# C turned in place, two groups' terms on GpSimd, and unread products in a scan layer

## The chip, the cores and the metric

The kernel runs on one core of one Trainium2 chip. A core has a matrix engine (TensorE, PE in the profile), three engines for element-wise work (VectorE or DVE, ScalarE or ACT, GpSimd or POOL), a queue engine that only issues transfers here (SyncE or SP), two kinds of memory near the engines (SBUF, and PSUM, into which TensorE writes), and DMA engines that move data to and from DRAM. Each engine works through its own list of instructions in order, and engines wait for one another by semaphores.

The metric is the device time of one execution in microseconds, as the median of several. A profiled execution leaves one record for nearly every instruction, and the span is the time from the first of them to the last.

## The reference, cut to what matters

The model is a chain of four layers on an image of 48 x 48 tokens with 768 channels: an attention block, a spectral layer, a scan layer, and a spectral layer again. The change touches the scan layer alone:

```python
B = silu(x @ W_B + b_B + B_bias)           # N = 64 channels x R = 4, per token
C = silu(x @ W_C + b_C + C_bias)
X = silu(x @ W_X + b_X)
alpha, gamma = sigmoid(x @ W_dec + b_dec), sigmoid(x @ W_lam + b_lam)
theta = x @ W_th + b_th
for i in range(12):
    inj = rope(B, theta * (i + 1)) * X
    H = conv3x3(H) + conv_b                # depthwise: one 3x3 filter per channel
    H = alpha * H + inj                    # i == 0
    H = alpha * H + (1 - gamma) * alpha * prev + gamma * inj
    prev = inj
out = silu((rope(C, theta * 12) * H) @ W_out + b_out)
```

`rope` turns pairs of channels by an angle: (a cos - b sin, a sin + b cos). Since the angle grows by theta from one iteration to the next, the sum of the terms that are added to H obeys a recurrence, s(i+1) = 2 cos(theta) s(i) - s(i-1), so that only the first two of them, `s0` and `s1`, are worked out by turning.

## The kernel before, in words

`scan_phase` holds the layer. Tokens lie on 112 of the 128 partitions (two image rows in 48 partitions each, the second at partition 64), so that the 48 rows make 24 pair-rows (`NPR`).

**Projections** (L1204 to L1294). A loop over eight column groups `q` takes three pair-rows each. For each pair-row, TensorE multiplies the tokens by all the weights (L1223): 357 columns (C, alpha, theta, X, gamma) and 256 columns (B), over six chunks of input channels, into one of three PSUM tiles `pss[0..2]`. Three of the six chunks come from `xh`, a tile that holds half of the layer's input for all tokens; the others come from tiles that `rows_back` makes. VectorE adds biases into two SBUF tiles, `za` (two buffers) and `g` (L1224). ACT applies silu to X, B and C (L1234), takes sin and cos (L1198, L1199) and sigmoids (L1250, L1251); each change of function costs a table load. VectorE turns B (`turn`, L1425, six operations with two temporaries `m0` and `m1`), writes the first H (L1260) and works out `s0` and `s1` (L1288, L1289, L1293, L1294), with ACT's products `u` (L1270). C, which is a part of `za`, and the cos and sin of 12 theta are written to DRAM (`c_d`, L1263, L1264). The last group's operations are held in program order by `pin`.

**Around the seam.** After the last group `x_close` gives back the memory of `xh` and of the projection weights. The output weights `wo`, `bo`, the filters `bands` of the groups 1 to 7 (group 0 has its own, loaded early) and `alr`, alpha spread over R, lie in the memory that has become free. SP issues their transfers in order.

**Diffusion** (L1316 to L1370). Iterations 1 to 11 times eight groups of eight channels (`gr`) make 88 steps. `step` issues: 64 passes of TensorE with the filters as band matrices (L1323) into `pss[gr % 4]`; VectorE's product with alpha (L1325, called mult in the prediction); VectorE's addition of `s` into H (L1327, called H); GpSimd's product t = 2 cos(theta) s (L1331); ACT's copy of t into the same PSUM tile (L1332). `after`, one step later, issues VectorE's s <- t - s (L1343, called sub), which reads t from PSUM. In the last iteration there is no next term; there the turned C is read from DRAM and multiplied with H (L1349), on GpSimd for seven groups and on VectorE for the last. On three of each four steps one more operation is issued from `turns`: for each of the eight `q`, C and the cos and sin are read from `c_d` (L1357, L1358), turned by six GpSimd operations (L1425), and written to DRAM as `cr_d`.

**Order.** The order on each engine is settled when the program is built: a scheduler places ready instructions by priority, except where `tc.keep_in_program_order` holds them. `keep_warm` (L128 to L133) is a helper that another stage uses already: it issues matmuls whose result nobody reads.

Of the kernel before, what the change touches and what calls it, by code (L numbers as in the profile page):

```python
# [12 lines left out]
F32 = mybir.dt.float32  # L13
F32R = mybir.dt.float32r
AF = mybir.ActivationFunctionType
ALU = mybir.AluOpType
# [4 lines left out]
P = 128  # L21
# [1108 lines left out]
def scan_phase(tc, ident, w, wts, rows_back, xh, x_close, c_d, cr_d, out_open):  # L1130
# [13 lines left out]
    nc = tc.nc  # L1144
    (b0_d, b1_d, cb_d, bands_d, wo_d, bo_d) = wts
    R4 = 3
# [8 lines left out]
    with tc.tile_pool(name="sc_s", bufs=1, side="left") as sp:  # L1155
# [9 lines left out]
        with (  # L1165
# [15 lines left out]
            with (  # L1181
# [27 lines left out]
                for q in range(NQ):  # L1209
# [50 lines left out]
                    V.tensor_tensor(H[:K, :, :, 1 + q * R4 : 1 + (q + 1) * R4], i03, over_r(ac, NN), ALU.add)  # L1260
                    pin(V.tensor_scalar(th, th, float(ITERS), None, ALU.mult))  # L1261
                    cs12 = sincos(th, q, "t12")
                    nc.sync.dma_start(c_d[:K, q, :NCR], c)  # L1263
                    nc.sync.dma_start(c_d[:K, q, NCR:].rearrange("p (s m) t -> p s m t", s=2), cs12)  # L1264
                    c1q = c1[:K, :, prs]
                    pin(V.tensor_scalar(c1q, cs[:, 0], 2.0, None, ALU.mult))

# [24 lines left out]
                    t1 = s1[:K, :, :, prs]  # L1292
                    V.tensor_tensor(t1, i03, over_r(bc, NN), ALU.mult)  # L1293
                    V.tensor_tensor(flat(t1), flat(t1), u, ALU.subtract)  # L1294
            x_close()
            wo, bo = out_weights()
            with (
# [5 lines left out]
                for gr in range(NG):  # L1303
# [2 lines left out]
                        nc.sync.dma_start(bands[:, (gr - 1) * GC : gr * GC], bands_d[:, ch])  # L1306
                    nc.scalar.copy(alr[:, ch], al[:, ch].unsqueeze(2).to_broadcast([P, GC, RR, NPR]))
                s = [s0, s1]
                half = GC * RR * NPR // 2

                def banks(v, gr):
# [2 lines left out]
                def step(it, gr):  # L1314

                    sc = s[it % 2]  # L1316
                    ch = slice(gr * GC, (gr + 1) * GC)
                    ps = pss[gr % 4]
                    for k in range(GC):
                        n = gr * GC + k  # L1320
                        cols = slice(k % 4 * RR * NPR, (k % 4 + 1) * RR * NPR)
                        for i, (r0, d) in enumerate(((0, 1), (HD, 1), (0, 0), (HD, 2))):
                            nc.tensor.matmul(ps[r0 : r0 + G, k // 4, cols], lhsT=bands[:, n - GC, i, :] if gr else bands0[:, n, i, :], rhs=H[:, n, :, d : d + NPR], start=i < 2, stop=i >= 2)  # L1323
                    pv = ps[:, :, :half]
                    V.tensor_tensor(pv, pv, banks(alr, gr), ALU.mult)  # L1325
                    by_bank = lambda v: v.rearrange("p (b n) r t -> p b (n r) t", b=2)
                    V.tensor_tensor(by_bank(H[:, ch])[:, :, :, 1 : 1 + NPR], pv.rearrange("p b (n t) -> p b n t", t=NPR), by_bank(sc[:, ch]), ALU.add)  # L1327
                    if it + 1 < ITERS:
                        t = tp.tile([P, GC, RR, NPR], F32, tag="t", name=f"t_{it}_{gr}")
                        m0 = (gr * GC) % NM  # L1330
                        GP.tensor_tensor(t, sc[:, ch], c1[:, m0 : m0 + GC].unsqueeze(2).to_broadcast([P, GC, RR, NPR]), ALU.mult)  # L1331
                        nc.scalar.copy(pv, t.rearrange("p (b n) r t -> p b (n r t)", b=2))  # L1332
                    else:
                        cr = tp.tile([P, NQ, GC * RR, R4], F32, tag="t", name=f"crg_{gr}")
                        nc.sync.dma_start(cr[:K], cr_d[:K, :, gr * GC * RR : (gr + 1) * GC * RR])
                        crs[gr] = cr

                def after(it, gr):

                    sn = s[(it + 1) % 2]  # L1340
                    if it + 1 < ITERS:
                        sb = banks(sn, gr)
                        V.tensor_tensor(sb, pss[gr % 4][:, :, :half], sb, ALU.subtract)  # L1343
                        return
                    nr = slice(gr * GC * RR, (gr + 1) * GC * RR)
                    hg = sn.rearrange("p n r t -> p (n r t)").rearrange("p (t n) -> p n t", t=NPR)
# [1 line left out]
                    by_q = lambda v: v.rearrange("p n (q t) -> p n q t", t=R4)  # L1348
                    (V if gr == NG - 1 else GP).tensor_tensor(by_q(hg[:K, nr]), by_q(Hd[:K]), crs[gr][:K].rearrange("p q n t -> p n q t"), ALU.mult)  # L1349

                def c_turned(q):


                    c, cr = (tp.tile([P, NCR, R4], F32, tag="t", name=f"{nm}_{q}")[:K] for nm in ("c", "cr"))
                    sc = tp.tile([P, 2 * NM, R4], F32, tag="sc", name=f"sc_{q}", bufs=2)[:K]
                    m = [tp.tile([P, NM, RR, R4], F32, tag=f"m{j}", name=f"m{j}_{q}", bufs=1)[:K] for j in range(2)]
                    nc.sync.dma_start(c, c_d[:K, q, :NCR])  # L1357
                    nc.sync.dma_start(sc, c_d[:K, q, NCR:])  # L1358
                    co, si = (sc[:, j * NM : (j + 1) * NM].unsqueeze(2).to_broadcast([K, NM, RR, R4]) for j in range(2))
                    yield from turn(GP, cr, c, co, si, m)  # L1360
                    yield lambda: nc.sync.dma_start(cr_d[:K, q], cr)

                crs = {}
                steps = [(it, gr) for it in range(1, ITERS) for gr in range(NG)]
                turns = (op for q in range(NQ) for op in c_turned(q))
                for i in range(len(steps) + 1):
                    if i < len(steps):
                        step(*steps[i])
                    if i % 4:
                        next(turns, int)()  # L1370
                    if i:
                        after(*steps[i - 1])
# [3 lines left out]
        with (  # L1376
# [24 lines left out]
            for half in range(2):  # L1401
                cols = slice(half * TB, (half + 1) * TB)
                for p2 in range(NPR // 2):
                    if half == 0 and p2 % 2 == 0:
                        turned(1, p2 // 2)
                    for t in range(2):
# [4 lines left out]
                        V.tensor_tensor(x3[:, pr, cols], ps[:K, :TB], bo[:, cols], ALU.add)  # L1411
                        nc.scalar.activation(x3[:, pr, cols], x3[:, pr, cols], AF.Silu)
                    yield


def turn(eng, out, in_, co, si, m):
# [12 lines left out]
def block_kernel(ctx: ExitStack, tc: tile.TileContext, a: dict):  # L1429
# [84 lines left out]
        return stack.enter_context(tc.tile_pool(name=name, bufs=1, side="right"))  # L1514

    wts = [a[k] for k in ("b_scan", "bias_scan", "conv_b", "bands", "W_out", "b_out")]
    c_d = dram.tile([P, 8, NN * RR + 2 * NM, 3], F32, tag="c_d", name="c_d")
    cr_d = dram.tile([P, 8, NN * RR, 3], F32, tag="cr_d", name="cr_d")

    def x_close():  # L1520
# [497 lines left out]
```

## Time and profile before

| | |
|---|---|
| median of 3 executions | 3582.45 us (3582.03 to 3585.97) |
| profiled execution | 3582.01 us, of it 3580.2 us span |
| busy: TensorE, VectorE, ACT, GpSimd | 3507.9, 2002.3, 1140.0, 679.5 us |
| projections, from about | 2823 us |
| last matmul of the projections, first of the diffusion | ends 2991.6, starts 3000.30 us |
| last matmul of the diffusion, about | 3247.2 us |

A line of a group reads: source line, engine, operation, output and inputs by the program's names, sizes, count, then busy time and mean duration in ns, then idle time of the engine just before and what ended it. A line of the instruction list reads: start in us, duration in us, engine, line, operation, and in brackets the idle time before it and what released it. A line of stretches reads: limits, length, then busy time with count of TensorE, its weight loads, VectorE, ACT and GpSimd, then the granted clock of TensorE (1 is full speed), the share of the DMA engines and GB/s. Records are pipelined: on VectorE the next instruction may start before the one ahead of it has ended, so a pace is read from starts.

### The profile page before, as it was taken

To read this page: it belongs to the slowest core of one execution; us is meant where nothing else is said; L and a number is where in the kernel's file an instruction comes from. 1 tells how busy PE (TensorE), PEld (TensorE's weight loads), DVE (VectorE), ACT (ScalarE), POOL (GpSimd) and SP (SyncE) were. 2 spreads that over 40 slices of the span, in tenths; PEclk is the share of its full clock that TensorE was granted. 3 is DMA by queue.
4 is the path that set the end of the run, shared out by engine and by line. 5 is a ranking of instruction groups with operands and counts; after the bars stand their busy time and mean duration, and the time that the engine had idled before them with its cause. 6 is when DMAs were issued, how large, how long until landed. Compare 5 with 4: busy or idle time off the path is not lost.

```text
span 3580.2 us, 52877 instructions
## 1 busy us (share of the span) xinstructions
PE 3507.9 (98%) x21238; PEld 2149.6 (60%) x21238; DVE 2002.3 (56%) x3015; ACT 1140.0 (32%) x1735; POOL 679.5 (19%) x566
## 2 busy tenths in 40 slices
PE   9999999999999999989999999999999998999997
PEld 5666554444444444555555555555578777996685
DVE  7644467776776776564243324232245478995454
ACT  1321255555555555103101210120023265223332
POOL 3211101111111110340000000000023303981131
PEclk9999999999999999999999999999999999999999
DMA  8555556655545443343346334534544403104356
GB/s 276 201 189 190 186 155 184 181 157 148 154 124 151 124 125 87 120 157 121 108 139 175 116 108 137 158 109 127 144 122 115 110 20 105 37 28 106 97 143 132
DMA packets 282167, 480.38 MB, mean 134 GB/s; under 512 B 39206, under 2 KB 235462, under 8 KB 275704
## 3 DMA queue, kind: packets, MB, share of 16 engines
q1 hardware_dynamic: 266568, 456.13, 43.9%
q10 hardware_dynamic: 15344, 20.75, 1.9%
q8 instruction: 171, 2.80, 0.3%
q14 instruction: 84, 0.69, 0.1%
HBM read 330.82 MB, written 145.98 MB: 133 GB/s over the span
## 4 chain that ended last, share of the span: by engine, by line
PE 90%; DVE 3%; DMA 3%; POOL 2%; ACT 1%; issue 1%; SPq 0%; ACTq 0%; POOLq 0%; DVEq 0%
PE p L996 14%; PE p L1059 13%; PE s L657 12%; PE av L688 12%; PE qk L375 6%; PE c L1223 4%; PE s L667 3%; PE c L1323 3%; PE v L180 3%; PE pj L180 2%; PE f_z L1666 2%; PE f_z L1667 2%; PE f_x L1631 2%; PE so L1410 2%; PE f_u L1682 2%; PE f_o L1645 1%
## 5 line engine op out<-in xcount | busy, mean ns | idle before, releaser
L677 DVE TENSOR_TENSOR acc<-acc,p 128x928 f32<-128x928 f32 (+1 forms) x480 | 561.1, 1169 | 258.8 <-ACT p L669 217.6
L669 ACT ACTIVATE p<-s 128x928 f32<-128x928 f32 (+1 forms) x540 | 505.9, 939 | 488.1 <-PE s L667 468.6
L657 PE MATMUL s<-qt,kv 64*128 64x464 f32 (+1 forms) x2160 | 520.8, 558 | 5.7 <-DMA qt<-q_d 5.7
L1059 PE MATMUL p<-w,h 128*128 128x384 f32 x1512 | 492.3, 487 | 0.0
L688 PE MATMUL av<-p,kv 128*64 128x464 f32 (+1 forms) x2160 | 442.6, 554 | 0.0
L1059 PEld LDWEIGHTS p<-w,h 128*128 128x128 f32 x1512 | 285.7, 190 | 198.8 <-issue 4.2
L667 PE MATMUL s<-bt,oneh 64*128 64x464 f32 (+1 forms) x1080 | 399.8, 729 | 0.8 <-DMA bt<-rh_d 0.8
L688 PEld LDWEIGHTS av<-p,kv 128*64 128x64 f32 x2160 | 147.0, 137 | 261.2 <-issue 248.8
L657 PEld LDWEIGHTS s<-qt,kv 64*128 64x128 f32 x2160 | 203.2, 187 | 162.0 <-issue 153.6
L996 PE MATMUL p<-x2nT,w 128*128 128x384 f32 x864 | 292.8, 489 | 4.2 <-POOL rr L1035 4.2
L1323 PE MATMUL c<-H,bands 128*48 128x96 f32 x5632 | 244.6, 247 | 10.9 <-DVE th L1261 8.3
L375 PE MATMUL qk<-xnT,wqk 128*128 128x384 f32 x756 | 249.8, 487 | 0.1
L1323 PEld LDWEIGHTS c<-H,bands 128*48 128x48 f32 x5632 | 234.8, 123 | 20.9 <-issue 8.7
L996 PEld LDWEIGHTS p<-x2nT,w 128*128 128x128 f32 x864 | 164.8, 191 | 120.8 <-POOL rr L1035 4.4
L996 PE MATMUL p<-xT,w 128*128 128x384 f32 x648 | 220.8, 486 | 0.0
L1035 POOL TENSOR_TENSOR rr<-rr,ml_b 128x1152 f32<-128x1152 f32 x12 | 31.8, 2649 | 944.7 <-DMA rr<-xr_d 828.3
L991 ACT ACTIVATE h<-h,ml_b 128x384 f32<-128x384 f32 x144 | 88.3, 614 | 345.8 <-DVE h L1011 173.6
L375 PEld LDWEIGHTS qk<-xnT,wqk 128*128 128x128 f32 x756 | 141.5, 190 | 93.1 <-issue 0.7
L1331 POOL TENSOR_TENSOR t<-s,c 128x768 f32<-128x768 f32 x80 | 144.4, 1828 | 180.8 <-DVE s L1294 168.2
L996 PEld LDWEIGHTS p<-xT,w 128*128 128x128 f32 x648 | 123.2, 190 | 85.8
L667 PEld LDWEIGHTS s<-bt,oneh 64*128 64x128 f32 x1080 | 106.8, 187 | 105.4 <-issue 103.3
L1666 PE MATMUL f_z<-f_w,f_o 97*96 97x96 f32 x800 | 134.2, 249 | 0.0
(334 smaller groups left out, 4594.0 us busy)
## 6 DMA issues: line engine op xcount, KB each, us to landing
w<-w1s_d SPq DMA_DIRECT2D x36, 768.0 KB
w<-w2s_d SPq DMA_DIRECT2D x36, 768.0 KB
w<-w1s_d SPq DMA_DIRECT2D x36, 576.0 KB
w<-in_mlp_w_dram SPq DMA_DIRECT2D x27, 768.0 KB
yu<-f_ys SPq DMA_DIRECT2D x48, 384.0 KB
wqk<-wqk_d SPq DMA_DIRECT2D x12, 1344.0 KB
bt<-rw_d SPq DMA_DIRECT2D x72, 174.0 KB
bt<-rh_d SPq DMA_DIRECT2D x72, 174.0 KB
```

Of the source, the lines that this page charges most:

```text
L180: nc.tensor.matmul(p[:, :TB], lhsT=rhs[n][:, c, t * P : (t + 1) * P], rhs=w[:, c, :], start=c == 0, stop=c == NC2 - 1)
L375: nc.tensor.matmul(p[:, :TB], lhsT=w[:, n, c, :], rhs=ops[sb][n][:, c, :], start=c == 0, stop=c == NC2 - 1)
L657: nc.tensor.matmul(ps[:, s, :n], lhsT=keys[pr % 2][rows, kt * P : (kt + 1) * P], rhs=held(c)[rows, :n], start=True, stop=False)
L667: nc.tensor.matmul(ps[:, s, :n], lhsT=oneh[rows, b % 2, :], rhs=bts[b // 2][rows, j, :n], start=False, stop=True)
L669: nc.scalar.activation(p, ps[:, :, :n], AF.Exp)
L677: nc.vector.tensor_tensor(probs[c], probs[c], p, ALU.add)
L688: nc.tensor.matmul(avs[c][rows, : size(c)], lhsT=vals[pr % 2][:, kt, rows], rhs=p[:, s, :], start=kt == 0, stop=kt == NT - 1)
L996: nc.tensor.matmul(p[:, :TB], lhsT=w[n][:, c, :], rhs=rhs[n][:, c, :], start=c == 0, stop=c == NC2 - 1)
L1059: nc.tensor.matmul(ps[t][:, :TB], lhsT=hs[left, f][:, t * P : (t + 1) * P], rhs=wt[:, f % KW2, :], start=f == 0, stop=f == NF2 - 1)
L1323: nc.tensor.matmul(ps[r0 : r0 + G, k // 4, cols], lhsT=bands[:, n - GC, i, :] if gr else bands0[:, n, i, :], rhs=H[:, n, :, d : d + NPR], ...
L1331: GP.tensor_tensor(t, sc[:, ch], c1[:, m0 : m0 + GC].unsqueeze(2).to_broadcast([P, GC, RR, NPR]), ALU.mult)
L1666: nc.tensor.matmul(out, lhsT=o1[:, j, 1:3, :].rearrange("c r h -> c (r h)"), rhs=w2t[:, b, 0, :], start=True, stop=False)
```

## The change

Four things change.

1. For the first seven column groups, C is turned in place in `za` by six GpSimd operations right after the sin and cos of 12 theta, with temporaries of the tags `m0` and `m1` that VectorE's turn uses too, and goes to `cr_d` by one transfer. The last group's C still goes through `c_d` and is turned by GpSimd during the diffusion, one operation on each fourth step.
2. For the groups 3 and 7 (`APART`), GpSimd itself forms s <- t - s in SBUF; ACT's copy and VectorE's sub are left out there.
3. Twelve matmuls of 128 x 384 into `pss[3]`, which nobody reads, stand between the projections and the diffusion. They read `xh`.
4. `c_d` shrinks to one column group.

Lines of the kernel after: matmuls L1331, mult L1333, H L1335, t L1339, GpSimd's s L1342, copy L1344, sub L1356, the product with turned C L1362, the in-place turn L1433, `turn` L1445, the call of `keep_warm` L1301.

```diff
@@ -1260,8 +1260,14 @@
                     V.tensor_tensor(H[:K, :, :, 1 + q * R4 : 1 + (q + 1) * R4], i03, over_r(ac, NN), ALU.add)
                     pin(V.tensor_scalar(th, th, float(ITERS), None, ALU.mult))
                     cs12 = sincos(th, q, "t12")
-                    nc.sync.dma_start(c_d[:K, q, :NCR], c)
-                    nc.sync.dma_start(c_d[:K, q, NCR:].rearrange("p (s m) t -> p s m t", s=2), cs12)
+                    if last:
+                        nc.sync.dma_start(c_d[:K, :NCR], c)
+                        nc.sync.dma_start(c_d[:K, NCR:].rearrange("p (s m) t -> p s m t", s=2), cs12)
+                    else:
+                        mc = [temp([NM, RR, R4], f"m{j}", f"c_{q}") for j in range(2)]
+                        for op in turn_in_place(GP, c, over_r(cs12[:, 0], NM), over_r(cs12[:, 1], NM), mc):
+                            op()
+                        nc.sync.dma_start(cr_d[:K, q], c)
                     c1q = c1[:K, :, prs]
                     pin(V.tensor_scalar(c1q, cs[:, 0], 2.0, None, ALU.mult))
 
@@ -1292,6 +1298,7 @@
                     t1 = s1[:K, :, :, prs]
                     V.tensor_tensor(t1, i03, over_r(bc, NN), ALU.mult)
                     V.tensor_tensor(flat(t1), flat(t1), u, ALU.subtract)
+            keep_warm(tc, pss[3][:, 0], xh[:, 0, :P], xh[:, 0, :384], 12)
             x_close()
             wo, bo = out_weights()
             with (
@@ -1306,6 +1313,7 @@
                         nc.sync.dma_start(bands[:, (gr - 1) * GC : gr * GC], bands_d[:, ch])
                     nc.scalar.copy(alr[:, ch], al[:, ch].unsqueeze(2).to_broadcast([P, GC, RR, NPR]))
                 s = [s0, s1]
+                APART = (3, 7)
                 half = GC * RR * NPR // 2
 
                 def banks(v, gr):
@@ -1329,7 +1337,11 @@
                         t = tp.tile([P, GC, RR, NPR], F32, tag="t", name=f"t_{it}_{gr}")
                         m0 = (gr * GC) % NM
                         GP.tensor_tensor(t, sc[:, ch], c1[:, m0 : m0 + GC].unsqueeze(2).to_broadcast([P, GC, RR, NPR]), ALU.mult)
-                        nc.scalar.copy(pv, t.rearrange("p (b n) r t -> p b (n r t)", b=2))
+                        if gr in APART:
+                            sn = s[(it + 1) % 2][:, ch]
+                            GP.tensor_tensor(sn, t, sn, ALU.subtract)
+                        else:
+                            nc.scalar.copy(pv, t.rearrange("p (b n) r t -> p b (n r t)", b=2))
                     else:
                         cr = tp.tile([P, NQ, GC * RR, R4], F32, tag="t", name=f"crg_{gr}")
                         nc.sync.dma_start(cr[:K], cr_d[:K, :, gr * GC * RR : (gr + 1) * GC * RR])
@@ -1339,8 +1351,9 @@
 
                     sn = s[(it + 1) % 2]
                     if it + 1 < ITERS:
-                        sb = banks(sn, gr)
-                        V.tensor_tensor(sb, pss[gr % 4][:, :, :half], sb, ALU.subtract)
+                        if gr not in APART:
+                            sb = banks(sn, gr)
+                            V.tensor_tensor(sb, pss[gr % 4][:, :, :half], sb, ALU.subtract)
                         return
                     nr = slice(gr * GC * RR, (gr + 1) * GC * RR)
                     hg = sn.rearrange("p n r t -> p (n r t)").rearrange("p (t n) -> p n t", t=NPR)
@@ -1348,25 +1361,25 @@
                     by_q = lambda v: v.rearrange("p n (q t) -> p n q t", t=R4)
                     (V if gr == NG - 1 else GP).tensor_tensor(by_q(hg[:K, nr]), by_q(Hd[:K]), crs[gr][:K].rearrange("p q n t -> p n q t"), ALU.mult)
 
-                def c_turned(q):
-
-
+                def c_turned():
+
+                    q = NQ - 1
                     c, cr = (tp.tile([P, NCR, R4], F32, tag="t", name=f"{nm}_{q}")[:K] for nm in ("c", "cr"))
-                    sc = tp.tile([P, 2 * NM, R4], F32, tag="sc", name=f"sc_{q}", bufs=2)[:K]
+                    sc = tp.tile([P, 2 * NM, R4], F32, tag="sc", name=f"sc_{q}", bufs=1)[:K]
                     m = [tp.tile([P, NM, RR, R4], F32, tag=f"m{j}", name=f"m{j}_{q}", bufs=1)[:K] for j in range(2)]
-                    nc.sync.dma_start(c, c_d[:K, q, :NCR])
-                    nc.sync.dma_start(sc, c_d[:K, q, NCR:])
+                    nc.sync.dma_start(c, c_d[:K, :NCR])
+                    nc.sync.dma_start(sc, c_d[:K, NCR:])
                     co, si = (sc[:, j * NM : (j + 1) * NM].unsqueeze(2).to_broadcast([K, NM, RR, R4]) for j in range(2))
                     yield from turn(GP, cr, c, co, si, m)
                     yield lambda: nc.sync.dma_start(cr_d[:K, q], cr)
 
                 crs = {}
                 steps = [(it, gr) for it in range(1, ITERS) for gr in range(NG)]
-                turns = (op for q in range(NQ) for op in c_turned(q))
+                turns = c_turned()
                 for i in range(len(steps) + 1):
                     if i < len(steps):
                         step(*steps[i])
-                    if i % 4:
+                    if i % 4 == 1:
                         next(turns, int)()
                     if i:
                         after(*steps[i - 1])
@@ -1411,6 +1424,13 @@
                         V.tensor_tensor(x3[:, pr, cols], ps[:K, :TB], bo[:, cols], ALU.add)
                         nc.scalar.activation(x3[:, pr, cols], x3[:, pr, cols], AF.Silu)
                     yield
+
+
+def turn_in_place(eng, v, co, si, m):
+    v = v.rearrange("p (j m r) t -> p j m r t", j=2, r=RR)
+    a, b = v[:, 0], v[:, 1]
+    for args in ((m[0], b, si, ALU.mult), (m[1], a, si, ALU.mult), (a, a, co, ALU.mult), (a, a, m[0], ALU.subtract), (b, b, co, ALU.mult), (b, b, m[1], ALU.add)):
+        yield lambda args=args: eng.tensor_tensor(*args)
 
 
 def turn(eng, out, in_, co, si, m):
@@ -1514,7 +1534,7 @@
         return stack.enter_context(tc.tile_pool(name=name, bufs=1, side="right"))
 
     wts = [a[k] for k in ("b_scan", "bias_scan", "conv_b", "bands", "W_out", "b_out")]
-    c_d = dram.tile([P, 8, NN * RR + 2 * NM, 3], F32, tag="c_d", name="c_d")
+    c_d = dram.tile([P, NN * RR + 2 * NM, 3], F32, tag="c_d", name="c_d")
     cr_d = dram.tile([P, 8, NN * RR, 3], F32, tag="cr_d", name="cr_d")
 
     def x_close():
```

`keep_warm`, which is called there, is unchanged:

```python
def keep_warm(tc, ps, left, right, n):
    k, m = left.shape
    for _ in range(n):
        tc.keep_in_program_order(tc.nc.tensor.matmul(ps[:m, : right.shape[1]], lhsT=left, rhs=right, start=True, stop=True))
```

## The prediction

> **What bounds the kernel now.** I read the page first (busy shares, costliest groups), then the table of stretches, the waits of 3000 to 3250 us, and the instructions one by one on both sides of 3000 us. The page's groups place the change: the diffusion is some 247 us of a span of 3580.2.
>
> ```profile
> L1323 PE MATMUL c<-H,bands 128*48 128x96 f32 x5632 | 244.6, 247 | 10.9 <-DVE th L1261 8.3
> ...
> L1331 POOL TENSOR_TENSOR t<-s,c 128x768 f32<-128x768 f32 x80 | 144.4, 1828 | 180.8 <-DVE s L1294 168.2
> ```
>
> The 8.3 us are TensorE's wait for the last column group's H; GpSimd's 168.2 us are its idle time through the projections. Steady diffusion, by stretches (PE, weight load, DVE, ACT, POOL):
>
> ```profile
> 3050.00:3100.00 50.00, 50.00 (x1162) 47.79 (x1160) 48.59 (x56) 14.54 (x19) 46.43 (x33) 1.00 0.12 34
> ```
>
> PE, VectorE and GpSimd all look full, so busy time cannot say which one sets the pace. Starts do. VectorE, steady state:
>
> ```profile
> 3042.68 0.95 DVE L1327 TENSOR_TENSOR H<-c,s 128x768 f32<-128x768 f32 x1
> 3043.54 0.96 DVE L1325 TENSOR_TENSOR c<-c,alr 128x768 f32<-128x768 f32 x1
> 3044.57 0.96 DVE L1343 TENSOR_TENSOR s<-c,s 128x768 f32<-128x768 f32 x1
> 3045.45 0.95 DVE L1327 TENSOR_TENSOR H<-c,s 128x768 f32<-128x768 f32 x1
> ```
>
> ```profile
> 3043.74 0.80 ACT L1332 COPY c<-t 128x768 f32<-128x768 f32 x1 [1.97 <-DVE H L1327]
> ```
>
> One step is a circle: H starts at 3042.68, its copy 1.06 later, the sub 0.83 after that (3044.57), the next H 0.88 later: 2.77 us. TensorE's 64 passes take 2.640 us when nothing holds them (the last four steps run so), so it spends some 0.13 us per step waiting for a PSUM tile. VectorE with ACT in its circle is the bound, narrowly.
>
> Ahead of it, the last group of the projections: TensorE ends at 2991.6 and starts again at 3000.30; between lie biases, silu, sin, turn and H on VectorE and ACT.
>
> ```profile
> 2988.15 1.71 ACT L1270 ACTIVATE u<-g,ga 112x256 f32<-112x256 f32 x3 [1.97 <-DVE s L1289]
> 2989.88 1.28 ACT L1234 ACT_TABLE_LOAD   x1
> 2992.66 0.21 ACT L1234 ACTIVATE za<-za 112x12 f32<-112x12 f32 x1 [1.50 <-DVE za L1224]
> ```
>
> The silu's table load is free now: it runs while ACT waits for `za`. VectorE there is nearly unbroken; its one pause before the last bias is 1.00 us:
>
> ```profile
> 2986.06 1.09 DVE L1293 TENSOR_TENSOR s<-i,bc 112x768 f32<-112x768 f32 x1
> 2987.03 1.09 DVE L1289 TENSOR_TENSOR s<-s,u 112x768 f32<-112x768 f32 x1
> ...
> 2989.89 1.10 DVE L1294 TENSOR_TENSOR s<-s,u 112x768 f32<-112x768 f32 x1 [0.50 <-ACT u L1270]
> 2991.99 0.63 DVE L1224 TENSOR_TENSOR za<-c,bias 112x357 f32<-112x357 f32 x1 [1.00 <-PE c L1223]
> ```
>
> **What the Trainium skill says.** "SBUF — State Buffer", section "Who interferes with whom": a VectorE instruction with two SBUF inputs contends with a GpSimd instruction that reads SBUF, one with a single SBUF input does not. The trace agrees both ways: `acc` L677 (two SBUF inputs) takes 1.09 us alone and 1.71 beside GpSimd, whose 128x384 op goes from 1.00 to 1.85; the diffusion's VectorE ops (one operand in PSUM) take 0.95 with GpSimd 93% busy.
>
> ```profile
> 607.96 1.85 POOL L147 TENSOR_TENSOR pw2p<-pw2p,pw2b 128x384 f32<-128x384 f32 x1
> ...
> 611.69 1.00 POOL L148 TENSOR_TENSOR pw2p<-pw2p 128x384 f32<-128x384 f32 x1
> ```
>
> "TensorE: Matmul & The Clock Gate", section "What's actually happening": after an idle window the clock is half until a busy window has passed. Here: granted clock 0.5 from 2994.2 to 3004.5, first diffusion step 4.67 us against 2.64.
>
> **The change part by part**, against the profiled execution (3582.01 us, of which 1.8 lie outside the span); the median of the runs shown is 0.4 above it.
>
> *Terms on GpSimd for groups 3 and 7.* Out: 20 copies (0.80) and 20 subs. In: 20 GpSimd ops; the trace has none with two full 128x768 operands, so t's pitch of 1.795 us is taken, with 1 and 2 times it as ends that do not matter: 10 ops per 8 steps are 17.95 us of 22.1. VectorE saves 20 x 0.88 = 17.6 us of work. But its program's order changes too. Before, each step is mult, sub of the step before, H. After, four steps run mult0 H0 sub0, mult1 H1, mult2 sub1 H2, mult3 sub2 H3: sub0 stands directly behind its own H0 and waits for the copy. Intervals from the trace: mult to own H 0.99 (3018.89 to 3019.88), H to mult 0.86, H to its own sub 1.06 + 0.83 = 1.89, sub to anything 0.88. H0 at 0; sub0 1.89; mult1 2.77; H1 3.76; mult2 4.62; sub1 5.65 (copy); H2 6.53; mult3 7.39; sub2 8.42; H3 9.30; mult0 10.16; H0 11.15. So 11.15 us for four steps, 2.79 a step, against 2.768 before and TensorE's 10.56. The time freed is spent waiting for the copy: +0.02 a step, not −0.13.
>
> *C turned in place.* Seven groups x six GpSimd ops (0.93 alone) move from the diffusion, where they filled gaps, into the projections, where GpSimd idled. The 42 round trips of c, sc and cr removed were hidden. Two costs. First, the ops run from the second sin (2986.2 in the seventh group) for 5.6 us and more, beside L1293, L1289 and L1294: 3 x (1.71 − 1.09) = 1.8 us on VectorE per group. The ends are nothing, and the full 6 x 0.93 = 5.6. Second, the silu that rewrites a `za` buffer now waits also for the GpSimd that turned it; its waits stand in one instruction ahead of the table load, so the 1.28 us load no longer starts early: about +1.2 per group from the third. If the load is hoisted after all, 0. Sum 3.0 per group; TensorE itself stays covered (each of its three PSUM tiles is wanted again only after two others' 6.2 us of matmuls: some 5 us to spare). VectorE's pauses ahead of the last bias of groups 5, 6, 7 are 1.56, 3.80, 1.00, which gives lateness 3.0 − 1.56 = 1.4, then 1.4 + 3.0 − 3.8 = 0.6, then 0.6 + 3.0 − 1.0 = 2.6. The last group's own load adds 1.2: the first H is 3.8 us late, with 1.2 and 6 as ends.
>
> *Unread products.* 24 passes x 0.322 (pitch of the same helper's at 3549 us) = 7.7 us fill TensorE's 8.34 us gap. They end near 2999.7; `wo`, `bo`, the bands and `alr` lie in memory they read, so their DMAs, which SP issues in order, start some 9 us later than now (2990.7). At the ~420 GB/s of now (1.87 us per 786 KB) the second group's bands land near 3006.5, then one set per 1.9 us: never later than a step needs. The clock gain is 4.67 − 2.64 = 2.03 us of TensorE. But `wo` and the bands hold step 1 to 3006.5 at best, and later PSUM releases by VectorE decide; counted 0.
>
> *Ramp.* Now VectorE stands 0.63 and 1.76 us before subs (3021.47, 3024.19) because t's queue behind turn ops. With one group left to turn, at step 9 TensorE is +4.6 us (3.8 late, bands and order 0.8). With fewer stalls behind it, it then runs at 2.64 for about 19 steps, −2.4. The other 59 steps lose 0.02 each, +1.2. Sum +3.4 us at the diffusion's end; what follows is unchanged. Profiled 3585.4, median **3586 us**.
>
> **Rivals.** (A) VectorE really is relieved: the copy comes sooner than 1.06 after H, sub0 does not stall and TensorE sets 2.640. Then 79 steps x 0.128 = −10.1, plus 3.4: about 3576. For it: VectorE's work falls to 9.7 us per four steps, under TensorE's 10.56. Against: the 1.06 is seen at every step. (B) This without the lateness (load hoisted, contention small, clock gain felt): −10 to −12, 3571: faster. (C) GpSimd holds VectorE for whole ops: 5.6 + 1.2 = 6.8 us per group exceed pauses and TensorE's slack from about 5 a group on. TensorE then stalls in groups 3 to 7: 8 to 12 us more than now, 3592. It is the slower side, decided by the stretch of L1288 to L1294. (D) No lateness, the order as worked out: −0.2, 3582.
>
> **How the numbers follow.** 0.2% (7.2 us: 3575.3 to 3589.6) is about what a measurement of this kernel can tell from no change. Forecast 0.46, A 0.15, B 0.08, C 0.19, D 0.12. Forecast, D and most of A lie within; the forecast's upper end (first H 6 us late, +5.8, or bands late besides) passes 3589.6 in part. So slower 0.27, within 0.58, faster 0.15. Range 3575 to 3594, which cuts B's and C's outer parts.
>
> **What would show it.** Right: steps at 2.79 with L1356 waiting for ACT directly behind H of groups 0 and 4; L1293, L1289 and L1294 above 1.09; the silu's load just ahead of it; the first matmul of diffusion near 3004; the first step at about 2.6. Wrong: steps at 2.64; the s ops unchanged; the load still in ACT's pause; bands landing behind their step; TensorE waiting inside L1223.

## The result, and the profile after

The changed kernel takes 3594.95 us as the median of ten runs, against 3584.99 us for ten of the kernel before: ratio 1.0025, 95% interval 1.0017 to 1.0033, so 6 to 12 us slower. The forecast of 3586 us stood 3.6 us above the median that was known, and its range ended 11.6 us above it; the difference of the two medians, 10.0 us, lies inside that range, near its end. By the forecast's own bounds of 0.2% either way this is its case "slower", to which it gave 0.27, and not "within", to which it gave 0.58 (though the interval reaches down to 1.0017). The sign was right, and so was most of the mechanism. The size was not: less than half of what was measured. The profiled execution of the changed kernel took 3588.7 us (span 3586.7), the one before 3582.01 (span 3580.2).

Spans are a blunt measure here. The work ahead of the scan layer, which is the same in all kernels, ended anywhere between 2822.6 and 2831.4 us. So I measure from the projections' first matmul. In the traces, the diffusion's first matmul starts 176.7 us after it in the kernel before and 183.2 after; its last one starts 423.7 and 430.6 us after it. The lateness is 6.5 us at the diffusion's start and 6.9 at its end. Nearly everything was lost in the projections and at the seam (the stretch between their last matmul and the diffusion's first); on balance the diffusion lost 0.4 us.

The page's groups for the diffusion (line, engine, operation, then busy time and mean ns, then the idle time before it and its releasers):

```profile
L1331 PE MATMUL c<-H,bands 128*48 128x96 f32 x5632 | 240.0, 246 | 10.8 <-DVE s L1356 4.1
...
L1339 POOL TENSOR_TENSOR t<-s,c 128x768 f32<-128x768 f32 x80 | 144.5, 1828 | 34.5 <-ACT c L1344 16.3
```

TensorE's longest idle time there is now a wait for VectorE's sub (4.1 of 10.8 us). GpSimd's one idle time of 168 us through the projections is broken up by the seven turns. Two stretches of the changed kernel's steady diffusion, then the second of them in the kernel before:

```profile
3050.00:3100.00 50.00, 49.72 (x1200) 49.34 (x1195) 44.25 (x49) 11.25 (x14) 49.22 (x29) 1.00 0.01 3
3100.00:3150.00 50.00, 48.62 (x1144) 47.01 (x1140) 45.23 (x51) 10.45 (x13) 45.03 (x25) 1.00 0.01 3
```

```profile
3100.00:3150.00 50.00, 49.80 (x1156) 47.53 (x1154) 48.45 (x54) 14.44 (x18) 44.80 (x32) 1.00 0.12 34
```

In the second stretch VectorE is less busy (45.2 of 50 us, before 48.45), and TensorE does fewer passes (1144, before 1156). VectorE's list shows why, and its waits from 2815 to 3260 us (in all, times, longest):

```profile
3147.79 0.95 DVE L1335 TENSOR_TENSOR H<-c,s 128x768 f32<-128x768 f32 x1
3148.65 0.96 DVE L1333 TENSOR_TENSOR c<-c,alr 128x768 f32<-128x768 f32 x1
3149.64 0.96 DVE L1335 TENSOR_TENSOR H<-c,s 128x768 f32<-128x768 f32 x1
3151.55 0.96 DVE L1356 TENSOR_TENSOR s<-c,s 128x768 f32<-128x768 f32 x1 [0.95 <-ACT c L1344]
3152.42 0.95 DVE L1333 TENSOR_TENSOR c<-c,alr 128x768 f32<-128x768 f32 x1
...
3158.96 0.95 DVE L1335 TENSOR_TENSOR H<-c,s 128x768 f32<-128x768 f32 x1
```

```profile
DVE s L1356 <- ACT c L1344: 20.8, 21, 1.9
```

From H of the last of four steps to the same of the next four, 3147.79 to 3158.96, are 11.17 us. The sub at 3151.55 stands directly behind its own H and waits 0.95 us for ACT's copy. Such waits were 4 with 3.8 us in all in the kernel before (3000 to 3250 us); now they are 21 with 20.8 us.

The seam, on ACT, VectorE and GpSimd:

```profile
2992.72 1.74 ACT L1276 ACTIVATE u<-g,ga 112x256 f32<-112x256 f32 x3 [1.98 <-DVE s L1295]
2996.78 1.28 ACT L1234 ACT_TABLE_LOAD   x1 [2.32 <-issue]
2998.07 0.21 ACT L1234 ACTIVATE za<-za 112x12 f32<-112x12 f32 x1
```

```profile
2990.61 1.08 DVE L1299 TENSOR_TENSOR s<-i,bc 112x768 f32<-112x768 f32 x1
2991.59 1.10 DVE L1295 TENSOR_TENSOR s<-s,u 112x768 f32<-112x768 f32 x1
...
2994.49 1.69 DVE L1300 TENSOR_TENSOR s<-s,u 112x768 f32<-112x768 f32 x1 [0.51 <-ACT u L1276]
...
2996.95 0.99 DVE L1244 COPY th<-za 112x96 f32<-112x96 f32 x1
2997.97 0.92 DVE L1118 TENSOR_SCALAR t_k<-th 112x96 f32<-112x96 f32 x1
```

```profile
2990.61 3.73 POOL L1433 TENSOR_TENSOR m_c<-za,t 112x384 f32<-112x384 f32 x2 [14.26 <-ACT t L1199]
2994.31 2.61 POOL L1433 TENSOR_TENSOR za<-za,t 112x384 f32<-112x384 f32 x2
```

ACT idles for 2.32 us ahead of the table load instead of loading in that time; the silu follows 1.29 us later. VectorE pays in three places: 0.6 us in the last s operation and 0.8 and 0.7 us in two tiny ones (the copy took 0.18 before). GpSimd pays more: its first two operations take 3.73 us together, where one alone takes 0.93. TensorE:

```profile
2906.13 1.13 PE L1787 MATMUL c<-f_iw,f_gt 128*128 128x96 f32 x8 [1.81 <-DVE x L66]
...
2994.93 7.90 PE L133 MATMUL c<-xh 128*128 128x384 f32 x24
3005.97 4.30 PE L1331 MATMUL c<-H,bands 128*48 128x96 f32 x64 [3.14 <-DVE th L1261]
3011.05 2.85 PE L1331 MATMUL c<-H,bands 128*48 128x96 f32 x64 [0.78 <-DMA bands<-in_bands_dram]
3015.74 5.98 PE L1331 MATMUL c<-H,bands 128*48 128x96 f32 x139 [1.84 <-DMA bands<-in_bands_dram]
```

It pauses 1.81 us inside the projections (0.44 us in the kernel before), ahead of the products of `rows_back`, then fills the gap with unread products, stands 3.14 us idle all the same, and has steps 1 and 2 wait for bands.

### The profile page after: what moved, and what is told of

The parts are those of the page before. It is cut to its first block, busy times and chain, and to the rows that moved or that the text cites. A ratio compares the mean times of both kernels' runs of the same rounds, so it can differ in the third digit from the quotient of the medians.

```text
span 3586.7 us, 52892 instructions
## 1 busy us (share of the span) xinstructions
PE 3511.8 (98%) x21262; PEld 2152.4 (60%) x21262; DVE 1995.5 (56%) x2995; ACT 1123.9 (31%) x1715; POOL 734.3 (20%) x586
## 5 line engine op out<-in xcount | busy, mean ns | idle before, releaser
L1331 PE MATMUL c<-H,bands 128*48 128x96 f32 x5632 | 240.0, 246 | 10.8 <-DVE s L1356 4.1
L1331 PEld LDWEIGHTS c<-H,bands 128*48 128x48 f32 x5632 | 234.1, 123 | 17.1 <-DVE s L1356 7.3
L1339 POOL TENSOR_TENSOR t<-s,c 128x768 f32<-128x768 f32 x80 | 144.5, 1828 | 34.5 <-ACT c L1344 16.3
```

## The experiments

All traces on one scale: time from the projections' first matmul to the start of the diffusion's first (seam), from there to the start of its last (diffusion), mean step from step 40 to 80, and how long TensorE's granted clock was half in mid-projections. The four times and lengths are of one profiled execution each, the ratio of all executions.

| kernel | seam, us | diffusion, us | step, us | half clock, us | ratio to before (95%) |
|---|---|---|---|---|---|
| before | 176.7 | 247.0 | 2.775 | 0 | |
| after | 183.2 | 247.4 | 2.800 | 0 | 1.0025 (1.0017 to 1.0033) |
| apart_only | 176.8 | 263.0 | 2.923 | 0 | 1.0045 (1.0028 to 1.0061) |
| inplace_only | 185.4 | 246.3 | 2.776 | 3.4 | 1.0023 (1.0014 to 1.0033) |
| warm_only | 176.8 | 252.2 | 2.771 | 0 | 1.0004 (0.9995 to 1.0013) |
| after_ordered | 185.6 | 238.6 | 2.640 | 3.4 | 0.9997 (0.9988 to 1.0006) |
| inplace_load | 179.2 | 246.0 | 2.770 | 0 | 1.0006 (0.9997 to 1.0015) |
| inplace_tiny | 176.7 | 244.6 | 2.776 | 0 | 0.9990 (0.9981 to 0.9999) |
| apart7_ordered | 176.7 | 246.5 | 2.782 | 0 | 1.0004 (0.9995 to 1.0013) |
| warm_bands0 | 176.8 | 246.1 | 2.776 | 0 | 0.9994 (0.9985 to 1.0002) |
| no_warm | 185.3 | 248.1 | 2.800 | 3.4 | 1.0027 (1.0016 to 1.0038) |
| after_load | 179.2 | 247.8 | 2.792 | 0 | 1.0013 (1.0004 to 1.0021) |
| mended | 183.2 | 237.6 | 2.640 | 6.8 | 0.9981 (0.9974 to 0.9988) |
| mended_late4 | 178.6 | 236.6 | 2.641 | 0 | 0.9978 (0.9966 to 0.9989) |

### Each part alone

**apart_only** is the kernel before with GpSimd's terms for groups 3 and 7.

```diff
+                APART = (3, 7)
+                        if gr in APART:
+                            sn = s[(it + 1) % 2][:, ch]
+                            GP.tensor_tensor(sn, t, sn, ALU.subtract)
+                        else:
                             nc.scalar.copy(pv, t.rearrange("p (b n) r t -> p b (n r t)", b=2))
...
-                        sb = banks(sn, gr)
-                        V.tensor_tensor(sb, pss[gr % 4][:, :, :half], sb, ALU.subtract)
+                        if gr not in APART:
+                            sb = banks(sn, gr)
+                            V.tensor_tensor(sb, pss[gr % 4][:, :, :half], sb, ALU.subtract)
```

> The kernel before with one part of the change alone: GpSimd forms the next term for groups 3 and 7. Theory of the order (a sub stands directly behind its own H and waits for the copy): first diffusion matmul unchanged near 3000.3 us, steady steps at 2.79 to 2.80 us against 2.77, end of the diffusion 0 to 2 us later than before. Rival (VectorE is relieved, TensorE sets 2.64): steps of 2.64 to 2.66 us, end of the diffusion 7 to 10 us earlier.

Both sides missed: 16.0 us more in the diffusion. Stretches, then GpSimd's list:

```profile
3050.00:3100.00 50.00, 44.11 (x1030) 42.33 (x1028) 40.06 (x45) 9.64 (x12) 46.94 (x32) 1.00 0.12 34
3100.00:3150.00 50.00, 46.97 (x1102) 45.26 (x1096) 43.32 (x49) 10.44 (x13) 48.26 (x33) 1.00 0.10 27
```

```profile
3105.59 0.99 POOL L1431 TENSOR_TENSOR cr<-cr,m 112x384 f32<-112x384 f32 x1
3106.54 1.84 POOL L1335 TENSOR_TENSOR s<-t,s 128x768 f32<-128x768 f32 x1
3108.46 7.15 POOL L1332 TENSOR_TENSOR t<-s,c 128x768 f32<-128x768 f32 x4
```

GpSimd is 94 and 97% busy while TensorE and VectorE thin out. Ten operations of 1.8 us and five or six turning ones of about 0.95 per eight steps are 23 to 24 us, which is 2.9 to 3.0 a step. So this part can't stand without the other, which takes the turning out of the diffusion; that neither expectation counted GpSimd's sum was my omission. It also gives the missing price: the operation with two full operands takes 1.84 us, like t.

**inplace_only** is the kernel before with the in-place turn: the changed kernel with `APART = ()` and without `keep_warm`.

> The kernel before with C turned in place in the projections alone, no unread products and no terms on GpSimd. Theory of the seam (GpSimd beside VectorE, TensorE stalls where rows_back waits, the silu's table load behind a wait): last matmul of the projections about 3 us later than before, first diffusion matmul 5 to 6 us later, whole run 4 to 6 us slower, the diffusion's own pace 2.77. Rival (the in-place turn is hidden and what was lost comes from the products and the order): first diffusion matmul within 1 us of before, whole run within 1.5 us of before.

The theory of the seam holds and its numbers were too small: the diffusion starts 8.7 us late (expected 5 to 6), TensorE leaves the projections 6.2 us late (expected 3), the pace is 2.776. Here TensorE's pause is longer still, and the granted clock was half for 3.4 us from 2909.3, just after it. TensorE and the VectorE copy it waited for:

```profile
2907.81 1.13 PE L1786 MATMUL c<-f_iw,f_gt 128*128 128x96 f32 x8 [2.51 <-DVE x L66]
```

```profile
2905.20 1.75 DVE L1295 TENSOR_TENSOR s<-s,u 112x768 f32<-112x768 f32 x1
2906.86 0.49 DVE L1224 TENSOR_TENSOR g<-c,bias 112x256 f32<-112x256 f32 x1
2907.22 0.54 DVE L66 COPY x<-c 128x384 f32<-128x384 f32 x1
```

The copy that empties `rows_back`'s PSUM bank stands in VectorE's list behind an s operation that takes 1.75 us beside GpSimd. In the kernel before it takes 1.07, and in the profiled execution of the changed kernel, beside GpSimd too, 1.04:

```profile
2904.22 1.04 DVE L1295 TENSOR_TENSOR s<-s,u 112x768 f32<-112x768 f32 x1
```

That is the 0.7 us by which TensorE's pause differs there (1.81 us against 2.51).

**warm_only** is the kernel before with the unread products.

```diff
+            keep_warm(tc, pss[3][:, 0], xh[:, 0, :P], xh[:, 0, :384], 12)
             x_close()
```

> The kernel before with the unread products alone. Theory (they hold wo and the bands back, and SP queues bands behind c_d's second transfer): first diffusion matmul unchanged near 3000.3 us, first step 2.64 us in place of 4.67, but step 1 and 2 wait for bands until about 3006 to 3008, net 0 to 3 us slower at the diffusion's end. Rival (the clock is the gain that was sought and is felt): diffusion's end 1.5 to 2 us earlier.

```profile
3004.16 2.85 PE L1324 MATMUL c<-H,bands 128*48 128x96 f32 x64 [0.62 <-DVE th L1261]
3013.05 12.16 PE L1324 MATMUL c<-H,bands 128*48 128x96 f32 x224 [6.04 <-DMA bands<-in_bands_dram]
```

The seam is unchanged and the first step takes 2.85 us instead of 4.67: the clock gain is real when nothing delays the first H. Then TensorE stands 6.04 us for bands. This trace loses 5.2 us in the diffusion, more than expected; the runs allow -1.8 to +4.7 us.

**no_warm** is the changed kernel without that one line.

> The changed kernel without the unread products. Theory (they hold the bands back by reading xh; the clock gain isn't felt): diffusion's first matmul as in the changed kernel within 1 us (183 us after the projections' first), no wait of TensorE for bands, step 2 some 2 us earlier, of which part is lost again before the end: 428 to 430 us from first projection to last diffusion matmul against 430.6. Rival (the products help by the clock): 432 us and more.

It missed: 433.4 us to the last matmul, where 428 to 430 were expected and the rival had named 432 and more. But 2.1 of the 2.8 us over the changed kernel lie ahead of the place where the products stood: this execution has the pause of 2.52 us and the half clock in mid-projections. The diffusion takes 248.1 us against 247.4, and the runs can't tell the two kernels apart (1.0027, and 1.0025 with the products). Its trace has no wait for bands and is at step 8 after 24.9 us, where the changed kernel needed 27.3; by step 32 it has lost all of that again (92.1 against 91.4). My reading, which no run tests apart: once VectorE's order sets the pace, a late band only uses up slack that VectorE would have taken later. As far as these runs can tell (some 3 to 4 us either way), the products neither help nor harm in the changed kernel.

### Causes taken away one at a time

**after_ordered** changes only VectorE's order in the diffusion.

```diff
-                    V.tensor_tensor(pv, pv, banks(alr, gr), ALU.mult)
+                    held = tc.keep_in_program_order if prev else lambda ins: ins
+                    held(V.tensor_tensor(pv, pv, banks(alr, gr), ALU.mult))
+                    if prev:
+                        after(*prev)
...
-                    V.tensor_tensor(by_bank(H[:, ch])[:, :, :, 1 : 1 + NPR], pv.rearrange("p b (n t) -> p b n t", t=NPR), by_bank(sc[:, ch]), ALU.add)
+                    held(V.tensor_tensor(by_bank(H[:, ch])[:, :, :, 1 : 1 + NPR], pv.rearrange("p b (n t) -> p b n t", t=NPR), by_bank(sc[:, ch]), ALU.add))
...
-                            V.tensor_tensor(sb, pss[gr % 4][:, :, :half], sb, ALU.subtract)
+                            tc.keep_in_program_order(V.tensor_tensor(sb, pss[gr % 4][:, :, :half], sb, ALU.subtract))
```

> The changed kernel whole, but VectorE's order in the diffusion held as mult, sub of the step before, H, so that a sub never stands directly behind its own H. Theory of the order: with groups 3 and 7 left out, four steps take 10.16 us of VectorE, less than TensorE's 10.56, so steady steps of 2.64 us; start of the diffusion as in the changed kernel (near 3006), its end some 8 to 9 us earlier than in the changed kernel, profiled run near 3580. Rival (GpSimd's terms or TensorE's own gaps set 2.80): steps stay at 2.79 to 2.80, run near 3588.

```profile
3146.48 0.96 DVE L1338 TENSOR_TENSOR H<-c,s 128x768 f32<-128x768 f32 x1
3147.90 0.97 DVE L1334 TENSOR_TENSOR c<-c,alr 128x768 f32<-128x768 f32 x1 [0.47 <-PE c L1331]
3148.78 0.95 DVE L1359 TENSOR_TENSOR s<-c,s 128x768 f32<-128x768 f32 x1
3149.64 0.95 DVE L1338 TENSOR_TENSOR H<-c,s 128x768 f32<-128x768 f32 x1
```

The next mult now lies between H and its sub, and VectorE waits for TensorE, which it does not do in the steady diffusion of the kernels before and after. TensorE runs at 2.640 us a step from step 9 on; the diffusion is 8.8 us shorter, from the order alone.

**inplace_load** adds to inplace_only a silu of one unused column, behind the last ACT operation of each group.

```diff
+                    if not last:
+                        tc.keep_in_program_order(nc.scalar.activation(spare, halfpi, AF.Silu))
```

> The in-place turn alone, as in inplace_only, plus a silu of one unused column at each group's end that brings silu's table into ACT before the wait. From the projections' first matmul to the diffusion's first it was 176.7 us before, 183.3 in the changed kernel, 185.4 in inplace_only. Theory that the table load behind the wait is half of the loss (1.27 us per group, from the third, in front of everything that VectorE does for that group): 178 to 181 us here, TensorE's pause ahead of rows_back's products under 1.5 us, run 2 to 4 us over before. Rival (GpSimd beside VectorE is the whole cause): 183 us and more, run as slow as inplace_only.

ACT at the seam:

```profile
2993.78 1.28 ACT L1303 ACT_TABLE_LOAD   x1
2995.08 0.20 ACT L1303 ACTIVATE spare<-halfpi 128x1 f32<-128x1 f32 x1
2996.04 0.21 ACT L1235 ACTIVATE za<-za 112x12 f32<-112x12 f32 x1 [0.76 <-issue]
```

The load fills ACT's pause. The seam falls from 185.4 to 179.2 us, and the half clock of 2909 is gone with TensorE's long pause (now 0.58 and 1.06 us).

**after_load** does the same in the changed kernel.

> The changed kernel whole, with silu's table brought in early and nothing else altered. If the late table load is the larger part of the late start (inplace_load against inplace_only): first diffusion matmul 179 to 180 us after the projections' first against 183.2, the order's 2.80 us per step unchanged, 426 to 427 us to the last diffusion matmul against 430.6, run about 4 to 5 us faster than the changed kernel and still 2 to 5 us slower than before. If contention alone makes the late start: 183 us, run as the changed kernel.

183.2 becomes 179.2, 430.6 becomes 427.0, the step stays near 2.80, and the runs go from 1.0025 to 1.0013: as expected. The late table load is 4.0 us of the 6.5 in these two traces (4.3 by the runs, some 3 us either way for each of them), and 2.5 are left. **inplace_tiny**, next, gives the same 2.5 us to GpSimd beside VectorE.

**inplace_tiny** leaves the turn of C out for seven groups, with one operation of 3 columns in place of six.

> As inplace_only, but GpSimd's six operations per group on C are replaced by one of 3 columns, so that C of seven groups is not turned: the waits stay, VectorE has no neighbour. Theory of two costs: the table load stays behind its wait (1.27 us per group), so 178 to 180 us from the projections' first matmul to the diffusion's first, s operations of VectorE 1.05 to 1.10 us all, no VectorE copy near 1 us. Rival (contention is the whole cause): 176.7 us as before. Second rival (the wait is the whole cause): 183 us and more.

176.7 us, which is the first rival. But the run didn't separate what it was to separate: with the tiny operation the silu waited for a transfer and VectorE alone, and the table load ran early again (2988.96, in ACT's pause). So against inplace_only it took both costs away at once. It does separate them against inplace_load, whose load is early too, and which differs by the six operations and the small silus: 179.2 us there, 176.7 here, so in these traces GpSimd's six operations per group beside VectorE cost 2.5 us. The in-place transfers and the fewer round trips, which stay here, cost nothing. It shows one thing besides: with only the last group's turning left in the diffusion and nothing else changed there, the diffusion is 2.4 us shorter than before. That is the gain of the early ramp, alone.

**warm_bands0** lets the unread products read the first group's bands instead of `xh`.

```diff
+            b0 = bands0.rearrange("p k i g -> p (k i g)")
+            keep_warm(tc, pss[3][:, 0], b0[:, :P], b0[:, :384], 12)
```

> The unread products alone, but reading the first group's bands, which stay, in place of xh. Theory (the memory they read is what held wo and the bands back): bands issued as before, first diffusion step 2.64 us, step 1 no later than its bands, end of the diffusion 0 to 2 us earlier than before relative to the projections' start (before 423.7 us, warm_only 429.0). Rival (the products themselves or SP's order cost): as in warm_only, 4 us or more later.

```profile
3003.95 5.98 PE L1325 MATMUL c<-H,bands 128*48 128x96 f32 x140 [0.63 <-DVE th L1261]
3010.61 4.99 PE L1325 MATMUL c<-H,bands 128*48 128x96 f32 x116 [0.68 <-issue]
```

Steps 0 and 1 run at full clock without a pause, no wait for a band shows, 246.1 us against 252.2. So what the products read was the fault in warm_only. The gain against before is 0.9 us in the trace; the runs can't tell it from nothing.

**apart7_ordered** is the kernel before with GpSimd's term for group 7 alone and VectorE's order held.

> The kernel before with GpSimd's term for group 7 alone and VectorE's order held as mult, sub of the step before, H; C is turned amid the diffusion as before. Theory: VectorE needs 7 x 2.77 + 1.86 = 21.25 us per eight steps (2.66 a step), GpSimd 16.2 for terms plus 5 turning operations of 0.93, 20.9: both near TensorE's 21.1, so steady steps of 2.64 to 2.70 us and a run 6 to 9 us faster than before (profiled 3573 to 3576). Rival (GpSimd becomes the bound as in apart_only, which needed 2.92 to 3.04): steps of 2.75 us and more, run not faster than before.

It missed: 2.782 us a step from 40 to 80, 2.70 from 32 to 56 and 2.84 from 56 to 80. GpSimd was 94 to 97% busy. My sum of 20.9 us per eight steps left out 7.3 us of waits for the transfers of the turned C, and that GpSimd can't start before the last group's s is done, 8.6 us after the diffusion's first matmul. From there its 80 terms, 10 s operations, 48 turning operations and these waits add up to 143.6 + 18.3 + 45.1 + 7.3 = 214.3 us, so to about 223 us with the start, where 80 steps of 2.64 last 211. Step 80 started at 225.4.

### A version that beats both

**mended** is the changed kernel with the three edits above: order, early table, other operand for the products.

> The changed kernel with three things altered: VectorE's order held as in after_ordered, silu's table brought in early as in inplace_load, and the unread products read the first group's bands as in warm_bands0. If the costs found are separate and add up: 179.2 us from the projections' first matmul to the diffusion's first (inplace_load), then some 238 us at 2.64 a step (after_ordered 238.7), 417 to 418 us in all against 423.7 before and 430.6 in the changed kernel; run 5 to 7 us faster than before. If late bands or GpSimd take their place, 421 us and more, no faster than before.

0.9981 (0.9974 to 0.9988): 7 us faster than before, 0.4% below the changed kernel. The diffusion came out as expected (237.6 us); the seam didn't (183.2, expected 179.2): in this execution TensorE paused 1.25 and 1.09 us at 2909 and 2912, and its clock was half for 6.8 us from 2912.9. At 3583.91 us it is one of the slowest of 17 executions (median 3579.92), so the trace shows less of the gain than the runs do.

**mended_late4** turns C of groups 2, 3, 6 and 7 in the diffusion, through `c_d` (8 groups again).

```diff
+    LATE = (2, 3, 6, 7)
...
-                    if last:
+                    if late:
...
-                    if i % 4 == 1:
+                    if i % 8 in (1, 4, 6):
```

> As mended, but C of the groups 2, 3, 6 and 7 is turned amid the diffusion as before, so that the in-place turn of these doesn't meet VectorE ahead of the rows_back products and of the last group. GpSimd then has 17.95 us of terms plus 2.6 operations of 0.93 per eight steps, 20.3 of TensorE's 21.1. Theory: 177 to 178 us to the diffusion's first matmul, then 238 to 240, 415 to 417 in all, run 6 to 9 us faster than before. Rival (clumps of turning operations on GpSimd hold the terms back, as in apart7_ordered): diffusion 242 us and more, slower than mended.

```profile
3050.00:3100.00 50.00, 49.21 (x1181) 48.50 (x1178) 45.43 (x51) 12.05 (x15) 49.30 (x32) 1.00 0.07 19
3100.00:3150.00 50.00, 50.00 (x1218) 50.00 (x1216) 48.33 (x55) 11.25 (x14) 49.37 (x31) 1.00 0.07 19
```

178.6 and 236.6 us, 415.2 in all, 8.5 less than before; ratio 0.9978 (0.9966 to 0.9989). TensorE is full for all of the second stretch although GpSimd is 99% busy. Whether it is better than mended the runs don't tell.

## Why the prediction was right and wrong

**The order of VectorE.** Right, and to the number: 11.15 us for four steps forecast, 11.17 measured; 2.79 a step forecast, 2.80 measured. after_ordered shows that the order is the cause and not the removed work. Rival A (TensorE sets 2.640) named a pace that this kernel can reach, but not in the order it was given.

**GpSimd beside VectorE.** The sum was near (1.8 us per group forecast, 0.6 + 0.8 + 0.7 = 2.1 at the end of the seventh), the place was not. Of L1293, L1289 and L1294 only the last was stretched in the changed kernel's seventh group; the other two kept their 1.08 to 1.10 us and held GpSimd up instead. The rest fell on a copy and a tensor_scalar of 96 elements with a single SBUF input, which my forecast counted as safe, since it gave the rule without its exception. The Trainium skill, "SBUF — State Buffer", section "Who interferes with whom", does name copy and tensor_scalar among those that can take the shared pair of ports in a 2-port mode, and says that whoever issues first holds it for the whole instruction. The copy's 0.99 us instead of 0.18 and the tensor_scalar's 0.92 instead of 0.21 fit that, being longer by somewhat less than one GpSimd operation (0.93); whether they ran in such a mode no run shows. GpSimd's 3.73 us for two operations, beside VectorE operations with two SBUF inputs, fit the rule that the forecast gave.

**The table load.** The mechanism was right (2996.78, directly ahead of the silu, behind 2.32 us of idle ACT), the size wrong. I counted 1.2 us per group in a ledger of VectorE's pauses and 1.2 for the last. Taken away (after_load), it gives 4.0 us, 2.6 of them by way of TensorE, as follows.

**"TensorE itself stays covered."** This is the step that failed. The five spare microseconds hold for the three PSUM tiles of the projections: no wait of L1223 for them shows. `rows_back` uses the two banks of `pss[3]`, and its matmuls stand in TensorE's own list between the projections' matmuls; they wait for copies (L64, L66) that VectorE and ACT reach only after what is late there. That wait was already 0.44 us before, so there was no slack. The changed kernel pauses 1.81, 0.74 and 0.78 us there, and TensorE leaves the projections 4.0 us later, counted from its first matmul there (172.35 against 168.37 us, to the end of the last; 2991.6, given above as that end in the kernel before, is the last one's start). With the early load (after_load, 169.74 us) it leaves them 1.4 us later. This is rival C's effect, TensorE stalling in the projections, at a third to a half of its price, and with another cause: not a VectorE that is full, but matmuls that wait for two copies. It carries the start of the diffusion past the end of the forecast's range for the first H (6 us): 6.5.

**The unread products.** Counting them at 0 came true within what the runs can tell (no_warm); the reason given, that VectorE decides later, fits but wasn't tested apart. "Never later than a step needs" was wrong, and bands landing behind their step were one of the forecast's own signs of being wrong. Step 1 waited 0.78 us for the second group's bands, which were issued at 3003.74, behind the products. SP issues the third to eighth group's bands behind the last group's second transfer to `c_d`, which waits for a sin that is itself late: it was issued at 3010.17, and step 2 waited 1.84 us. And little clock was gained: the first step's passes took 4.30 us (4.67 before, 2.64 to 2.85 with full clock), with the granted clock half for 3.4 us from 3007.2, after TensorE had still stood 3.14 us behind the products.

**The ramp.** Forecast 3.8 us late at the first matmul, 4.6 at step 9, then 2.4 regained by step 28, then 1.2 lost, 3.4 at the end. Measured, from the projections' first matmul: 6.5, 7.8 at step 9, 5.5 at step 28, 6.9 at the end. So the shape is right (2.3 regained, 1.4 lost); of the 3.5 us too many at the end, 2.7 are there at the first matmul already, and 0.5 more come by step 9, where the late bands lie.

**Trace and runs.** The runs say +9.0 us (ratio 1.0025 of 3585), the profiled pair +6.7; the profiled execution of the changed kernel is the fastest of its ten. In three kernels that share the turn in place and the late table load (inplace_only, after_ordered, no_warm), the s operation ahead of `rows_back`'s copy took 1.75 or 1.76 us, TensorE paused for 2.51 to 2.53 us, and 3.4 us of half clock followed; in the profiled execution of the changed kernel it took 1.04, with a pause of 1.81 and no half clock. Up to there the four kernels have the same lines. That many of the changed kernel's other executions had the longer pause would explain the difference. It was not shown, since those left no trace, and the mean clocks listed with them (0.988 to 0.990) are too coarse: 3.4 us of half clock move such a mean by 0.0005.

## What to carry to other kernels

Work taken from an engine shortens nothing while that engine's next instruction waits for the same neighbour: look at what moves up behind what in its list, and hold the order so that other work lies between a producer and its consumer. Before moving work onto an idle engine, follow what its new waits stand in front of (a table load on ACT, a copy that empties a PSUM bank), and ask of each matmul in TensorE's list separately how long its release can slip. And ask of filler work what memory it reads and who is waiting for that memory.

## What the runs showed of the hardware

- Pauses of TensorE of 2.51 to 2.53 us were followed by 3.4 us of half clock in all three executions that had them; one of 1.81 us and a pair of 0.58 and 1.06 us were not; a pair of 1.25 and 1.09 us went with 6.8 us of it. All the half-clock stretches inside the scan layer lasted about 3.4 us or a multiple of it (6.8, 10.2, 13.7). That the pauses caused them is likely from this, not shown.
- Beside GpSimd a VectorE copy of 112 x 96 took 0.99 us instead of 0.18 and a tensor_scalar 0.92 instead of 0.21; two GpSimd operations of 0.93 us took 3.73 beside two s operations of VectorE that kept 1.08 and 1.10. One and the same s operation took 1.04 us in one execution and 1.75 or 1.76 in others, beside the same GpSimd operations.
- Where the silu of `za` had to wait for a transfer, VectorE and GpSimd together, its table load of 1.28 us came after the wait; where it waited for a transfer and VectorE, the load ran ahead in the idle time.
